# One DRAM row per token for both experts' outputs, added by the indirect stores, and the rows' steps placed anew

## The chip, the cores and the metric

The kernel runs on one core of one Trainium2 chip. The metric is device time in microseconds (us) of the whole program; the median over several executions counts. A profile is one execution taken with the hardware profiler. Its engines are PE (matrix multiply, with PEld for its weight loads), DVE (vector), ACT (scalar), POOL (GpSimd) and SP (which here only issues DMAs).

## What is computed

The input x is 16 rows of 512 tokens of 256 channels, float32. Two residual blocks follow each other; `_ln` is a layer norm without weights:

```python
x = x + _ln(attn(_ln(x)))      # an RWKV mix: three projections, a scan over the 512 tokens, a division, a projection
x = x + _ln(moe(_ln(x)))       # mixture of experts

def moe(xt):                                   # xt: 8192 tokens x 256
    scores = softmax(xt @ gate_w.T + gate_b)   # 8 experts
    top_w, top_i = top_k(scores, 2)            # two experts for each token
    y = sum over the two of top_w * expert_e(xt)           # 256 -> 256 -> 256, silu gate, biases
    z = silu(xt @ ws1.T + bs1) * (xt @ ws3.T + bs3) @ ws2.T + bs2   # the shared expert, 512 wide
    return y + z
```

## The kernel before

**Stages.** Rows b = 0 to 15 go through `front(b)` (layer norm, transposes `pt`, projections `pk`, `pv`, `pr`, the scans, the division `sb`) and `back(b)` (projection `po`, second norm, gate scores `pg`, positions `pc`). `back` ends by scattering each token's normalised row twice, once for each of its experts, into the DRAM array `xbuf`, sorted by expert: eight indirect stores from POOL at L500 per row. Each such row carries in two extra columns where its result is to go (R_TO) and its gate weight (R_GATE). `select(b)` then finds which blocks of 256 sorted rows are full; there are 71 blocks in all.

**Blocks.** A block passes a software pipeline, one stage per `push`. `block_load` reads 256 rows `xg` and the expert's weights `we` (898 KB) by SP (L589, L591). `block_turn` transposes (`px`), `block_hidden` computes `pa`, `pb`, `sil` and `he`, and `block_out` makes `pq` and `ye`. `block_store` scales `ye` by the gate on ACT (L640) and stores 2 x 128 rows by two indirect DMAs from POOL (L642) into `ybuf`, at the row that R_TO gives. `xg` has five buffers and `ye` three, so the load for a block waits until the stores of the block five ahead of it have landed. In before `ybuf` has two rows for each token, one per expert, and no store ever meets another's row; stores that belong to padding have a row number out of range and are dropped.

**The shared expert.** It runs in steps of its own (`shared`, two `hs` matrices, then `pz`). The first ten rows are done beside the row stage and go to DRAM (`zs`, written after L715 adds the bias bs2 on DVE). The last six are done in the tail.

**The tail.** After the last row come the remaining blocks, and then 32 half rows: `fetch` and `fetch_experts` read the half's `x2`, `zs` and `ybuf` rows; `gather` adds z and the two expert rows on DVE (L780, L781), takes moments, and asks POOL for the scales; `conclude` normalises on ACT and adds x2 on POOL (L792); `put` writes `out`. For the 12 halves whose z comes straight from PSUM, `add_bias` adds bs2 on POOL (L772).

**Order.** PE, DVE, ACT and SP run in an order written out by hand. Each step of a row has a place on a time axis of 10 units per row (`ROW`, with exceptions for rows 0 to 3 in `ROWS`); `BESIDE` and `PHASE` place shared steps and pushes, `Z_AFTER` and `K_LAST` place the tail's halves. All steps are sorted by place and issued so. POOL's order follows the same places through `pool` and `store`, which chain each POOL instruction behind the one ahead.

```python
at(PERIOD * b + when[n], step)          # a step of row b at its place
in_order()                              # all steps, sorted by place
```

Of the kernel before, what the change touches and what calls it, by code (L numbers as in the profile page):

```python
# [14 lines left out]
P = 128  # L15
# [14 lines left out]
PERIOD = 10.0  # L30
ROW = {'x': -8.0, 'sum': -5.0, 'sq': -2.0, 'xn': -0.5, 'pt': -0.49, 'mix': 1.0, 'r': 3.0, 'k0': 3.01, 'k1': 3.02, 'd0': 4.01, 'f0': 7.5, 'd1': 7.51, 'f1': 8.8, 'po0': 9.9, 'po1': 12.9, 'x2': 12.91, 'stc': 13.01, 'xr': 17.5, 'pu': 19.51, 'pg': 19.52, 'pc': 20.53, 'sel': 21.5}
ROWS = {1: {'x2': 13.11, 'stc': 13.21, 'xr': 17.7, 'pu': 19.71, 'pg': 19.72, 'pc': 20.73, 'sel': 21.7}, 3: {'po1': 12.4}, 0: {'k0': 2.81, 'pc': 21.53, 'sel': 21.54}, 2: {}}
CONST_AT = -4.5
# [4 lines left out]
TURN_FIRST = True  # L38
PHASE = 0.5
BESIDE = [6, 8]  # L40
EARLY = 8
LAST_BESIDE = 6
XR_COPY = 'pool'
FILL = [0.5, 0.6, 0.7, 1.5, 1.6, 2.5]
Z_AFTER = [0, 3]
K_FIRST = 1.2
K_LAST = 31.7
FINE = 1
FETCH = 4.8
FETCH_Y = 2.6  # L50
BIAS = 1.5
GATHER = -0.1
GATHER_Z = 0.1
CONCLUDE = 1.5
PUT = 2.2

# [5 lines left out]
def kernel(  # L62
# [63 lines left out]
    xbuf = dram.tile([NR, RW], F32, tag="xbuf", name="xbuf")  # L126
    ybuf = dram.tile([2 * N, C], F32, tag="ybuf", name="ybuf")


    AFTER = mybir.DependencyInfo(mybir.DependencyClass.Sync, mybir.DependencyReason.DATA)  # L130
    stored = {"x": [], "y": []}

# [64 lines left out]
    def the_constants():  # L197


        def counted(shape, pattern, name, by_partition=0):  # L200
# [12 lines left out]
        counted([P, 2], [[P, 2]], "lane", 1)  # L213
        counted([P, NT], [[2 * P, NT]], "token", 2)

        blank = const.tile([P, RW], F32, tag="blank", name="blank")
        nc.vector.memset(blank, 0.0)
        nc.vector.tensor_scalar(
            blank[:, R_TO : R_TO + 1].bitcast(U32), consts["token"][:, 0:1], float(2 * N), None, ALU.add
        )  # L220
# [162 lines left out]
    xTs = {}  # L383
    x2t = {}
    selected = {}

    def back(b):
# [32 lines left out]

        if b < B - 2:
            nc.sync.dma_start(out=x2s[b], in_=x2t.pop(b).rearrange("p t c -> p (t c)"))
        xr = []
        for k in range(2):
            r = wk.tile([P, NT, RW], F32, tag=f"xr{k}", name=f"xr{k}_{b}")
            pool(nc.gpsimd.memset(r[:, :, R_END:], 0.0))
            if k == 0:
                for t in range(NT):
                    normalise(r[:, t, 0:C], x2[:, t, :], s, t)
            pool(  # L430
                nc.gpsimd.tensor_scalar(
                    r[:, :, R_TO].bitcast(U32), consts["token"], float(2 * T * b + k), None, ALU.add
                )
            )
            xr.append(r)
# [75 lines left out]
    def select(b):  # L511
# [50 lines left out]
        if last:  # L562
# [10 lines left out]
            for e in range(E):  # L573
                for i in range(2):
                    j = nc.gpsimd.indirect_dma_start(
                        out=xbuf[:, :],
                        out_offset=bass.IndirectOffsetOnAxis(ap=padu[:, e, i : i + 1], axis=0),
                        in_=consts["blank"][:, :],
                        in_offset=None,
                    )  # L580
                    store("x", j)
        selected[b] = (atu, S, stored["x"])
        stored["x"] = []

    def block_load(atu, s, q, names):
# [50 lines left out]
    def block_store(i):  # L636

        y, xg = i["y"], i["xg"]
        for t in range(2):
            nc.scalar.mul(y[:, t, :], y[:, t, :], xg[:, t, R_GATE : R_GATE + 1])  # L640
        for t in range(2):
# [4 lines left out]
                in_offset=None,  # L646
                bounds_check=2 * N - 1,
                oob_is_err=False,
            )
            store("y", j)  # L650

# [73 lines left out]
    HOMES = (  # L725
        [("x", f"m{n}", f"{a}0") for n, a in (("r", "ek"), ("k", "ekv"), ("v", "sa"))]
        + [(f"xr{k}", n, a) for k, n, a in ((0, "d", "sb0"), (1, "xx", "ek1"))]
        + [("we", None, a) for a in ("ekv1", "sa1", "sb1")]
    )
    WAYS = len(HOMES)  # L730
    fetched = {}
    in_use = {}

    def fetch(i):
# [5 lines left out]
        cs = slice(2 * j * C, (2 * j + 2) * C)  # L740
        home, other, a = HOMES[k]
        if home == "we":
            both = wp.tile([P, WE], F32, tag="we", name=f"in{n}")
            ys, x2 = both[:, 0 : 4 * C], both[:, 4 * C : 6 * C]
        elif home == "x":
            ys = xp.tile([P, NT, C], F32, tag="x", name=f"in{n}", bufs=3).rearrange("p t c -> p (t c)")
            x2 = None
        else:
            ys = wk.tile([P, NT * RW], F32, tag=home, name=f"in{n}")[:, 0 : 4 * C]
            x2 = None  # L750
        if b in x2t:
            i["x2"] = x2t[b][:, 2 * j : 2 * j + 2, :]
        else:
            if x2 is None:
                x2 = wk.tile([P, 2 * C], F32, tag=other, name=f"inx{n}")
            nc.sync.dma_start(out=x2, in_=x2s[b][:, cs])
            i["x2"] = x2.rearrange("p (t c) -> p t c", t=2)
# [4 lines left out]
        i["ys"] = ys.rearrange("p (t k c) -> p t k c", t=2, k=2)  # L762

    def fetch_experts(i):
        b, j = i["b"], i["j"]
        mine = ybuf[2 * T * b : 2 * T * (b + 1), :].rearrange("(t p k) c -> p t k c", p=P, k=2)
        load("y", nc.sync.dma_start(out=i["ys"], in_=mine[:, 2 * j : 2 * j + 2]), stored["y"])

    def add_bias(i):
        if not i["z"]:  # L770
            y = i["ys"][:, :, 0, :]
            pool(nc.gpsimd.tensor_tensor(y, y, bs2t[:, None, :].to_broadcast([P, 2, C]), ALU.add))  # L772

    def gather(i):
# [3 lines left out]
        for p in range(parts):  # L778
            ts = slice(p * 2 // parts, (p + 1) * 2 // parts)
            nc.vector.tensor_add(acc[:, ts], i.get("pz", acc)[:, ts], ys[:, ts, 0, :])  # L780
# [4 lines left out]
            i["s"].append(scales(mv[:, :, 0], mv[:, :, 1], w, 2 // parts))  # L785

    def conclude(i):
        acc, b, j = i["acc"], i["b"], i["j"]
        if not i["fine"]:
            for t in range(2):  # L790
                normalise(acc[:, t, :], acc[:, t, :], i["s"][0], t)
            pool(nc.gpsimd.tensor_tensor(acc, acc, i["x2"], ALU.add))  # L792
            return
        for t in range(2):
            normalise(acc[:, t, :], acc[:, t, :], i["s"][t], 0)
            nc.vector.tensor_add(acc[:, t, :], acc[:, t, :], i["x2"][:, t, :])
# [239 lines left out]
```

## Time and profile before

| quantity | value |
|---|---|
| median of 6 runs | 1175.76 us (1175.6 to 1177.78) |
| the profiled execution's own time | 1171.52 us |
| its span, first to last instruction | 1169.8 us |
| mean granted PE clock | 0.957 |
| PE busy | 1073.6 us (92%) |
| DVE busy | 766.0 us (65%) |
| ACT busy | 533.7 us (46%) |
| POOL busy | 593.4 us (51%) |
| software queue (POOL's DMAs) | 37.00 MB, 8.7% of 16 engines |
| hardware queue (SP's DMAs) | 144.64 MB, 36.8% of 16 engines |

The table gives the page's first and third part. Busy shares are averages over stages that have different limits, so the text reads them stage by stage. A row of a group gives busy time and the mean of one instruction in ns; then the idle time of its engine just before, and what ended it.

### The profile page before, as it was taken

Reading aid. Unit: us, or ns where it says so; the run is one execution under the profiler, and the core shown is the slowest. Engines: PE = TensorE matmul, PEld = TensorE weight load, DVE = VectorE, ACT = ScalarE, POOL = GpSimd, SP = SyncE. Lnnn points to the kernel's source line nnn. Section 1 sums busy time; section 2 is a strip of 40 time slices with the busy share of each in tenths; the row PEclk is TensorE's granted clock in tenths of the full one; section 3 lists DMA queues with packets and bytes.
Section 4 is the critical chain, followed back from the end, with each engine's and each line's share of the span. In section 5 each row is a group of like instructions: output and inputs, shape, how many; then the busy total and the mean of one; then the engine's idle time right before and its main releaser. Section 6 shows DMA issues by size and latency. Waiting matters only on the chain.

```text
span 1169.8 us, 15070 instructions
## 1 busy us (share of the span) xinstructions
PE 1073.6 (92%) x4228; PEld 752.3 (64%) x4228; DVE 766.0 (65%) x1878; ACT 533.7 (46%) x1135; POOL 593.4 (51%) x877
## 2 busy tenths in 40 slices
PE   5678899899999999999999999999996999999993
PEld 2344565666677677767767686777665888746552
DVE  4787486877768586977769687874322222268885
ACT  3246154555637474655647464552412333333332
POOL 2235425354555546465555655554363233359897
PEclk9779899999989999999999989999987999999997
DMA  4001314334444452635445354444424666478883
GB/s 149 22 25 47 107 62 156 110 136 161 150 171 150 156 183 95 208 129 177 143 159 174 138 198 148 147 158 146 150 108 144 217 215 227 169 249 298 307 268 118
DMA packets 81124, 183.65 MB, mean 157 GB/s; under 512 B 10077, under 2 KB 44911, under 8 KB 81040
## 3 DMA queue, kind: packets, MB, share of 16 engines
q1 hardware_dynamic: 66480, 144.64, 36.8%
q0 software_dynamic: 13840, 37.00, 8.7%
q10 hardware_dynamic: 720, 1.06, 0.3%
q8 instruction: 33, 0.54, 0.2%
q14 instruction: 51, 0.42, 0.1%
HBM read 124.57 MB, written 59.92 MB: 158 GB/s over the span
## 4 chain that ended last, share of the span: by engine, by line
PE 61%; DVE 10%; POOL 9%; issue 9%; ACT 6%; DMA 2%; another core or an unknown queue 2%; SPq 0%; POOLq 0%; DVEq 0%; ACTq 0%
PE pq L629 8%; PE pa L613 8%; PE pz L703 6%; PE pb L613 6%; PE hs_pa L688 5%; PE hs_pb L688 5%; PE pr L338 5%; PE pk L338 5%; PE pv L338 4%; PE po L398 4%; PE pg L453 2%; POOL acc L792 2%; PE px L599 2%; ACT xn L270 2%
## 5 line engine op out<-in xcount | busy, mean ns | idle before, releaser
L642 POOL DMA_INDIRECT ybuf<-ye,xg x142 | 157.7, 1111 | 192.1 <-ACT ye L640 123.4
L500 POOL DMA_INDIRECT xbuf<-xr,place x128 | 128.4, 1003 | 148.0 <-DVE rest L497 101.5
L629 PE MATMUL pq<-we,he 128*128 128x256 f32 x568 | 138.6, 387 | 14.9 <-DVE he L618 14.5
L613 PE MATMUL pa<-xgT,we 128*128 128x256 f32 x568 | 134.6, 380 | 0.0
L613 PE MATMUL pb<-xgT,we 128*128 128x256 f32 x568 | 134.2, 379 | 0.0
L703 PE MATMUL pz<-ws2t,hs 128*128 128x256 f32 x512 | 125.9, 401 | 7.5 <-DVE hs L694 7.5
L618 DVE SCALAR_TENSOR_TENSOR he<-pb,we,sil 128x256 f32<-128x256 f32 x142 | 61.9, 478 | 108.0 <-PE pb L613 56.7
L616 ACT ACTIVATE sil<-pa,we 128x256 f32<-128x256 f32 x142 | 59.7, 472 | 155.2 <-PE pa L613 136.3
L629 PEld LDWEIGHTS pq<-we,he 128*128 128x128 f32 x568 | 102.4, 192 | 33.9 <-DVE he L618 20.7
L688 PE MATMUL hs_pa<-xT,ws1t 128*128 128x512 f32 x256 | 122.4, 601 | 0.3 <-ACT x L270 0.3
L703 PEld LDWEIGHTS pz<-ws2t,hs 128*128 128x128 f32 x512 | 102.2, 202 | 31.7 <-DVE hs L694 11.0
L688 PE MATMUL hs_pb<-xT,ws3t 128*128 128x512 f32 x256 | 120.4, 592 | 0.0
L613 PEld LDWEIGHTS pa<-xgT,we 128*128 128x128 f32 x568 | 108.3, 191 | 14.8
L613 PEld LDWEIGHTS pb<-xgT,we 128*128 128x128 f32 x568 | 107.9, 190 | 14.7
L371 DVE RECIPROCAL sb<-sb 128x512 f32<-128x512 f32 x32 | 107.3, 3353 | 1.1
L270 ACT ACTIVATE x<-po,nb_b,rs_b 128x256 f32<-128x256 f32 x64 | 30.9, 564 | 157.5 <-POOL nb_b L265 154.4
L688 PEld LDWEIGHTS hs_pb<-xT,ws3t 128*128 128x128 f32 x256 | 48.6, 190 | 61.5 <-issue 57.4
L245 DVE BATCH_NORM_STATS2 st_c<-x 128x6 f32<-128x256 f32 x64 | 26.3, 411 | 91.3 <-POOL x L413 90.5
L398 PE MATMUL po<-wa,g 128*128 128x256 f32 x256 | 72.9, 434 | 6.2 <-DVE g L376 6.2
L688 PEld LDWEIGHTS hs_pa<-xT,ws1t 128*128 128x128 f32 x256 | 48.7, 194 | 45.3 <-issue 42.2
L270 ACT ACTIVATE acc<-acc,nb_d,rs_d 128x256 f32<-128x256 f32 x64 | 35.1, 595 | 82.0 <-POOL nb_d L265 82.0
L633 DVE TENSOR_TENSOR ye<-pq,we 128x512 f32<-128x512 f32 x71 | 48.5, 683 | 36.7 <-PE pq L629 34.0
(179 smaller groups left out, 1928.7 us busy)
## 6 DMA issues: line engine op xcount, KB each, us to landing
we<-in_we SPq DMA_DIRECT2D x71, 898.0 KB
xg<-xbuf SPq DMA_DIRECT2D x71, 258.0 KB
in<-ybuf SPq DMA_DIRECT2D x32, 512.0 KB
x<-in_x SPq DMA_DIRECT2D x16, 512.0 KB
out<-acc SPq DMA_DIRECT2D x31, 256.0 KB
x2s<-x SPq DMA_DIRECT2D x14, 512.0 KB
zs<-z SPq DMA_DIRECT2D x10, 512.0 KB
acc<-zs SPq DMA_DIRECT2D x20, 256.0 KB
```

What stands on the lines that cost most here:

```text
L270: nc.scalar.activation(dst, src, AF.Identity, bias=nb[:, t : t + 1], scale=rs[:, t : t + 1])
L338: nc.tensor.matmul(p, w[:, c, o * P : (o + 1) * P], r, start=(c == 0), stop=(c == NC - 1))
L371: nc.vector.reciprocal(sb, sb)
L398: nc.tensor.matmul(p[:, i, :], g[:, c, t * P : (t + 1) * P], woT[:, c, :], start=(c == 0), stop=(c == NC - 1))
L500: i = nc.gpsimd.indirect_dma_start(out=xbuf[:, :], out_offset=bass.IndirectOffsetOnAxis(ap=place[:, t, k : k + 1], axis=0), in_=xr[k][:, t ...
L613: nc.tensor.matmul(p[:, f, :], w[:, k : k + P], xgT[:, c, :], start=(c == 0), stop=(c == NC - 1))
L616: nc.scalar.activation(s[:, f, :], pp[0][:, f, :], AF.Silu, bias=w[:, O_B1 + f : O_B1 + f + 1])
L618: nc.vector.scalar_tensor_tensor(h[:, f, :], pp[1][:, f, :], w[:, O_B3 + f : O_B3 + f + 1], s[:, f, :], ALU.add, ALU.mult)
L629: nc.tensor.matmul(p[:, t, :], h[:, f, t * P : (t + 1) * P], w[:, k : k + C], start=(f == 0), stop=(f == NF - 1))
L642: j = nc.gpsimd.indirect_dma_start(out=ybuf[:, :], out_offset=bass.IndirectOffsetOnAxis(ap=xg[:, t, R_TO : R_TO + 1].bitcast(U32), axis=0) ...
L688: nc.tensor.matmul(p, w[:, c, f * P : (f + 1) * P], xT[:, c, :], start=(c == 0), stop=(c == NC - 1))
L703: nc.tensor.matmul(p[:, i, :], h[f][:, t * P : (t + 1) * P], ws2t[:, f, :], start=(f == 0), stop=(f == NS - 1))
```

## The change

It gives `ybuf` one row for each token (plus 256 for padding). `clear(b)`, a new step at place 2.05 of each row, writes the bias bs2 into that row's 512 tokens by one SP DMA. The indirect stores of `block_store` no longer write but add (`compute_op=ALU.add`), and two blocks may meet in one row, so the stores of one block are ordered behind those of the block ahead, and only the two stores within a block are free of each other. The half rows then read one expert row instead of two and add it once; `add_bias` is gone, and z goes to DRAM without the bias, copied by ACT. `ROW`, `ROWS`, `BESIDE`, `PHASE`, `Z_AFTER`, `K_LAST` and `PUT` have new values. The switch `OUT_ADD` is False, so what hangs on it does not run.

```diff
-ROW = {'x': -8.0, 'sum': -5.0, 'sq': -2.0, 'xn': -0.5, 'pt': -0.49, 'mix': 1.0, 'r': 3.0, 'k0': 3.01, 'k1': 3.02, 'd0': 4.01, 'f0': 7.5, 'd1': 7.51, 'f1': 8.8, 'po0': 9.9, 'po1': 12.9, 'x2': 12.91, 'stc': 13.01, 'xr': 17.5, 'pu': 19.51, 'pg': 19.52, 'pc': 20.53, 'sel': 21.5}
-ROWS = {1: {'x2': 13.11, 'stc': 13.21, 'xr': 17.7, 'pu': 19.71, 'pg': 19.72, 'pc': 20.73, 'sel': 21.7}, 3: {'po1': 12.4}, 0: {'k0': 2.81, 'pc': 21.53, 'sel': 21.54}, 2: {}}
+ROW = {'x': -7.5, 'sum': -4.5, 'sq': -2.0, 'xn': -0.5, 'pt': -0.49, 'mix': 1.0, 'r': 3.5, 'k0': 3.01, 'k1': 3.02, 'd0': 4.01, 'f0': 7.5, 'd1': 7.51, 'f1': 8.8, 'po0': 11.9, 'po1': 12.9, 'x2': 12.91, 'stc': 12.92, 'xr': 17.5, 'pu': 19.51, 'pg': 19.72, 'pc': 20.73, 'sel': 21.7}
+ROWS = {1: {'x': -8.3, 'sum': -5.5, 'sq': -2.5, 'xn': -1.0, 'pt': -0.99, 'r': 5.5, 'd0': 5.51, 'x2': 13.11, 'stc': 13.21, 'xr': 17.7, 'pu': 19.71}, 3: {'po1': 12.4, 'x2': 12.41}, 0: {'xn': 0.0, 'pt': 0.01, 'k0': 2.81, 'pc': 21.53, 'sel': 21.54}, 2: {}}
...
-PHASE = 0.5
-BESIDE = [6, 8]
+PHASE = 0.2
+BESIDE = [5, 9, 3]
...
-Z_AFTER = [0, 3]
+Z_AFTER = [2, 3]
...
-K_LAST = 31.7
+K_LAST = 32.2
...
-BIAS = 1.5
+OUT_ADD = False
+CLEAR_AT = 2.05
...
-PUT = 2.2
+PUT = 2.0
...
-    ybuf = dram.tile([2 * N, C], F32, tag="ybuf", name="ybuf")
+    ybuf = dram.tile([N + BS, C], F32, tag="ybuf", name="ybuf")
...
+    def clear(b):
+
+        todo = [ybuf[T * b : T * (b + 1), :]] + ([ybuf[N:, :]] if b == 0 else [])
+        for a in todo:
+            n = a.shape[0] // P
+            i = nc.sync.dma_start(out=rows(a), in_=bs2t[:, None, :].to_broadcast([P, n, C]))
+            for g in adds:
+                tc.declare_no_dep(i.ins, group=g, reason="rows of no earlier block")
...
     def block_store(i):
 
         y, xg = i["y"], i["xg"]
+
+        adds.append(f"y_adds{i['q']}")
...
-                bounds_check=2 * N - 1,
-                oob_is_err=False,
+                compute_op=ALU.add,
             )
-            store("y", j)
+            store(None, j)
+            tc.declare_no_dep(j.ins, group=adds[-1], reason="tokens of their own")
+            tc.add_to_no_dep_group(adds[-1], j.ins)
...
-            nc.vector.tensor_tensor(
-                z[b][:, 2 * j : 2 * j + 2, :], p, bs2t[:, None, :].to_broadcast([P, 2, C]), ALU.add
-            )
+            nc.scalar.copy(z[b][:, 2 * j : 2 * j + 2, :], p)
...
-        mine = ybuf[2 * T * b : 2 * T * (b + 1), :].rearrange("(t p k) c -> p t k c", p=P, k=2)
-        load("y", nc.sync.dma_start(out=i["ys"], in_=mine[:, 2 * j : 2 * j + 2]), stored["y"])
-
-    def add_bias(i):
-        if not i["z"]:
-            y = i["ys"][:, :, 0, :]
-            pool(nc.gpsimd.tensor_tensor(y, y, bs2t[:, None, :].to_broadcast([P, 2, C]), ALU.add))
+        mine = rows(ybuf[T * b : T * (b + 1), :])
+        nc.sync.dma_start(out=i["ys"], in_=mine[:, 2 * j : 2 * j + 2])
...
-            nc.vector.tensor_add(acc[:, ts], i.get("pz", acc)[:, ts], ys[:, ts, 0, :])
-            nc.vector.tensor_add(acc[:, ts], acc[:, ts], ys[:, ts, 1, :])
+            nc.vector.tensor_add(acc[:, ts], i.get("pz", acc)[:, ts], ys[:, ts])
...
+        at(PERIOD * b + CLEAR_AT, lambda b=b: clear(b))
```

More of the change, by code (lines that the diff above doesn't have):

```diff
@@ L38 @@
 TURN_FIRST = True
-PHASE = 0.5
-BESIDE = [6, 8]
+PHASE = 0.2
+BESIDE = [5, 9, 3]
 EARLY = 8
 LAST_BESIDE = 6
-XR_COPY = 'pool'
+XR_COPY = "pool"
 FILL = [0.5, 0.6, 0.7, 1.5, 1.6, 2.5]
-Z_AFTER = [0, 3]
+Z_AFTER = [2, 3]
 K_FIRST = 1.2
-K_LAST = 31.7
+K_LAST = 32.2
 FINE = 1
@@ L126 @@
     xbuf = dram.tile([NR, RW], F32, tag="xbuf", name="xbuf")
-    ybuf = dram.tile([2 * N, C], F32, tag="ybuf", name="ybuf")
+    ybuf = dram.tile([N + BS, C], F32, tag="ybuf", name="ybuf")
     AFTER = mybir.DependencyInfo(mybir.DependencyClass.Sync, mybir.DependencyReason.DATA)
-    stored = {"x": [], "y": []}
+    stored = {"x": []}
+    adds = []
     BEHIND = mybir.DependencyInfo(mybir.DependencyClass.NoSync, mybir.DependencyReason.DATA)
@@ L147, in store @@
             tail["stores"].append(ins.ins.name)
+        if what is None:
+            return
         tc.declare_no_dep(ins.ins, group=f"{what}_stores", reason="rows of their own")
@@ L213, in the_constants @@
         counted([P, 2], [[P, 2]], "lane", 1)
-        counted([P, NT], [[2 * P, NT]], "token", 2)
-        blank = const.tile([P, RW], F32, tag="blank", name="blank")
+        counted([P, NT], [[P, NT]], "token", 1)
+        blank = const.tile([P, BS // P, RW], F32, tag="blank", name="blank")
         nc.vector.memset(blank, 0.0)
         nc.vector.tensor_scalar(
-            blank[:, R_TO : R_TO + 1].bitcast(U32), consts["token"][:, 0:1], float(2 * N), None, ALU.add
+            blank[:, :, R_TO].bitcast(U32), consts["token"][:, 0 : BS // P], float(N), None, ALU.add
         )
@@ L384 @@
     x2t = {}
+    kept = {}
     selected = {}
@@ L419, in back @@
         yield
-        if b < B - 2:
+        if OUT_ADD:
+            kept[b] = nc.sync.dma_start(out=rows(out[b]), in_=x2t.pop(b)).ins.name
+        elif b < B - 2:
             nc.sync.dma_start(out=x2s[b], in_=x2t.pop(b).rearrange("p t c -> p (t c)"))
@@ L431, in back @@
                 nc.gpsimd.tensor_scalar(
-                    r[:, :, R_TO].bitcast(U32), consts["token"], float(2 * T * b + k), None, ALU.add
+                    r[:, :, R_TO].bitcast(U32), consts["token"], float(T * b), None, ALU.add
                 )
@@ L577, in select @@
                         out_offset=bass.IndirectOffsetOnAxis(ap=padu[:, e, i : i + 1], axis=0),
-                        in_=consts["blank"][:, :],
+                        in_=consts["blank"][:, i, :],
                         in_offset=None,
@@ L725 @@
     HOMES = (
-        [("x", f"m{n}", f"{a}0") for n, a in (("r", "ek"), ("k", "ekv"), ("v", "sa"))]
-        + [(f"xr{k}", n, a) for k, n, a in ((0, "d", "sb0"), (1, "xx", "ek1"))]
-        + [("we", None, a) for a in ("ekv1", "sa1", "sb1")]
+        [("x", f"{a}0") for a in ("ek", "ekv", "sa")]
+        + [("xr0", "sb0"), ("xr1", "ek1")]
+        + [("we", a) for a in ("ekv1", "sa1", "sb1")]
     )
     WAYS = len(HOMES)
-    fetched = {}
     in_use = {}
@@ L740, in fetch @@
         cs = slice(2 * j * C, (2 * j + 2) * C)
-        home, other, a = HOMES[k]
+        home, a = HOMES[k]
         if home == "we":
             both = wp.tile([P, WE], F32, tag="we", name=f"in{n}")
-            ys, x2 = both[:, 0 : 4 * C], both[:, 4 * C : 6 * C]
         elif home == "x":
-            ys = xp.tile([P, NT, C], F32, tag="x", name=f"in{n}", bufs=3).rearrange("p t c -> p (t c)")
-            x2 = None
-        else:
-            ys = wk.tile([P, NT * RW], F32, tag=home, name=f"in{n}")[:, 0 : 4 * C]
-            x2 = None
+            both = xp.tile([P, NT, C], F32, tag="x", name=f"in{n}", bufs=3).rearrange("p t c -> p (t c)")
+        else:
+            both = wk.tile([P, NT * RW], F32, tag=home, name=f"in{n}")
+        two = both[:, 0 : 4 * C].rearrange("p (n t c) -> p n t c", n=2, t=2)
+        i["ys"] = two[:, 0]
         if b in x2t:
             i["x2"] = x2t[b][:, 2 * j : 2 * j + 2, :]
[L753 to L757, printed above, removed]
+        elif not OUT_ADD:
+            i["x2"] = two[:, 1]
+            nc.sync.dma_start(out=both[:, 2 * C : 4 * C], in_=x2s[b][:, cs])
         acc = wk.tile([P, 2 * C], F32, tag=a, name=f"acc{n}")
@@ L761, in fetch @@
         i["acc"] = acc.rearrange("p (t c) -> p t c", t=2)
-        i["ys"] = ys.rearrange("p (t k c) -> p t k c", t=2, k=2)
     def fetch_experts(i):
         b, j = i["b"], i["j"]
-        mine = ybuf[2 * T * b : 2 * T * (b + 1), :].rearrange("(t p k) c -> p t k c", p=P, k=2)
-        load("y", nc.sync.dma_start(out=i["ys"], in_=mine[:, 2 * j : 2 * j + 2]), stored["y"])
-    def add_bias(i):
-        if not i["z"]:
-            y = i["ys"][:, :, 0, :]
-            pool(nc.gpsimd.tensor_tensor(y, y, bs2t[:, None, :].to_broadcast([P, 2, C]), ALU.add))
+        mine = rows(ybuf[T * b : T * (b + 1), :])
+        nc.sync.dma_start(out=i["ys"], in_=mine[:, 2 * j : 2 * j + 2])
     def gather(i):
@@ L785, in gather, with onto @@
             i["s"].append(scales(mv[:, :, 0], mv[:, :, 1], w, 2 // parts))
+    def onto(i, t):
+        b, j = i["b"], i["j"]
+        ts = slice(2 * j + t.start, 2 * j + t.stop)
+        d = nc.gpsimd.dma_start(out=rows(out[b])[:, ts], in_=i["acc"][:, t], accum_op=ALU.add)
+        tc.add_manual_dep(d.ins, kept[b], AFTER, reason="what it adds to")
+        pool(d)
     def conclude(i):
@@ L791, in conclude @@
                 normalise(acc[:, t, :], acc[:, t, :], i["s"][0], t)
-            pool(nc.gpsimd.tensor_tensor(acc, acc, i["x2"], ALU.add))
+            if not OUT_ADD:
+                pool(nc.gpsimd.tensor_tensor(acc, acc, i["x2"], ALU.add))
             return
@@ L795, in conclude @@
             normalise(acc[:, t, :], acc[:, t, :], i["s"][t], 0)
-            nc.vector.tensor_add(acc[:, t, :], acc[:, t, :], i["x2"][:, t, :])
-            nc.sync.dma_start(out=rows(out[b])[:, 2 * j + t], in_=acc[:, t, :])
+            if OUT_ADD:
+                onto(i, slice(t, t + 1))
+            else:
+                nc.vector.tensor_add(acc[:, t, :], acc[:, t, :], i["x2"][:, t, :])
+                nc.sync.dma_start(out=rows(out[b])[:, 2 * j + t], in_=acc[:, t, :])
     def put(i):
@@ L801, in put @@
         if not i["fine"]:
-            nc.sync.dma_start(out=rows(out[b])[:, 2 * j : 2 * j + 2], in_=i["acc"])
+            if OUT_ADD:
+                onto(i, slice(0, 2))
+            else:
+                nc.sync.dma_start(out=rows(out[b])[:, 2 * j : 2 * j + 2], in_=i["acc"])
         del in_use[i["k"] % WAYS]
@@ L888, in blank_block @@
             out=rows(xbuf[E * STRETCH :, :]),
-            in_=consts["blank"][:, None, :].to_broadcast([P, BS // P, RW]),
+            in_=consts["blank"],
         )
@@ L945 @@
             halves.append((n, dict(b=rows_done + r, j=f - NS, z=False)))
-    kept = [(b, j) for b in range(rows_done) for j in range(NT // 2)]
-    for i, (b, j) in enumerate(kept):
-        halves.append((K_FIRST + (K_LAST - K_FIRST) * i / (len(kept) - 1), dict(b=b, j=j, z=True)))
+    spilt = [(b, j) for b in range(rows_done) for j in range(NT // 2)]
+    for i, (b, j) in enumerate(spilt):
+        halves.append((K_FIRST + (K_LAST - K_FIRST) * i / (len(spilt) - 1), dict(b=b, j=j, z=True)))
     halves.sort(key=lambda h: h[0])
@@ L958 @@
         at(max(n - FETCH_Y, free, 0.001) + 0.001, lambda i=i: fetch_experts(i))
-        at(max(n - BIAS, free, 0.001) + 0.002, lambda i=i: add_bias(i))
         at(n + (GATHER_Z if not i["z"] else GATHER), lambda i=i: gather(i))
```

## The prediction

> **What bounds the kernel now.** I read the page first, then the busy times cut by stage, because the shares of the whole span mix stages with different limits. Columns: stretch, its length, busy time (instructions) of PE, PEld, DVE, ACT, POOL; granted PE clock; DMA share; GB/s.
>
> ```profile
> 0.00:60.00 60.00, 34.64 (x80) 16.93 (x80) 35.79 (x72) 20.66 (x52) 15.30 (x46) 0.89 0.28 90
> ...
> 60.00:115.00 55.00, 46.04 (x138) 26.50 (x139) 45.69 (x84) 28.97 (x66) 24.89 (x44) 0.83 0.08 31
> ...
> 537.00:590.00 53.00, 51.90 (x237) 39.58 (x235) 39.54 (x100) 29.72 (x66) 28.10 (x41) 1.00 0.47 160
> ...
> 890.00:995.00 105.00, 102.46 (x477) 85.29 (x476) 27.44 (x51) 36.08 (x82) 31.21 (x32) 0.99 0.62 213
> ...
> 1140.00:1170.00 30.00, 10.58 (x39) 8.00 (x37) 15.85 (x34) 7.82 (x14) 21.00 (x36) 0.75 0.38 122
> ```
>
> PE is the limit in a middle row (51.9 of 53) and in the block stretch of the tail (102.5 of 105). It isn't at the start (34.6 of 60) and at the end (10.6 of 30, where POOL has 21). So time can be won by removing PE's waits in the rows, by a shorter start, and by a shorter end. It can be lost where stores pace the blocks. PE's waits in the full rows (220 to 870 us) are almost all at one place:
>
> ```profile
> PE pc L481 <- DVE sc L476: 9.1, 9, 1.2
> PE pc L481 <- DVE mine L475: 2.7, 1, 2.7
> ```
>
> For SP, the list of waits in the block stretch (915 to 1025) names the stores:
>
> ```profile
> SPq L589 <- DMA ybuf<-ye,xg: 49.9, 13, 5.5
> ```
>
> Then the timeline of that stretch, which is where the change adds its wait:
>
> ```profile
> 941.09 0.97 POOL L642 DMA_INDIRECT ybuf<-ye,xg  x1 [3.83 <-ACT ye L640]
> ...
> 942.37 0.97 POOL L642 DMA_INDIRECT ybuf<-ye,xg  x1 [0.30 <-issue]
> ...
> 946.30 0.38 SPq L589 DMA_DIRECT2D xg<-xbuf  x1
> ...
> 947.17 0.97 POOL L642 DMA_INDIRECT ybuf<-ye,xg  x1 [3.83 <-ACT ye L640]
> ...
> 948.45 0.98 POOL L642 DMA_INDIRECT ybuf<-ye,xg  x1 [0.31 <-issue]
> ...
> 953.09 0.38 SPq L589 DMA_DIRECT2D xg<-xbuf  x1
> ```
>
> POOL issues a block's two stores in 2.25 us (941.09 to 943.34), then idles 3.83 us: blocks come every 6.08 us. SP's next `xg` load goes out when those stores have landed, so its issue dates the landing: 2.96 us after the stores' issue ended, then 3.66. The eleven such distances from 939.66 to 1003.42 run from 2.4 to 6.6 and average 4.1.
>
> Last the timeline of the end:
>
> ```profile
> 1143.35 0.70 PE L703 MATMUL pz<-ws2t,hs 128*128 128x256 f32 x2 [1.04 <-DVE hs L694]
> ...
> 1147.70 7.57 PE L703 MATMUL pz<-ws2t,hs 128*128 128x256 f32 x26 [3.64 <-DVE hs L694]
> ...
> 1154.43 1.26 POOL L772 TENSOR_TENSOR in<-in,bs2t 128x512 f32<-128x512 f32 x1
> ...
> 1155.72 0.42 DVE L780 TENSOR_TENSOR acc<-pz,in 128x256 f32<-128x256 f32 x1 [1.18 <-POOL in L772]
> ...
> 1162.04 0.83 DVE L796 TENSOR_TENSOR acc<-acc,x 128x256 f32<-128x256 f32 x1 [1.02 <-ACT acc L270]
> ```
>
> PE waits for a DVE that is behind, and the last half then waits for POOL's bias add. PE ends at 1155.27, the last add at 1162.87.
>
> **The rows: pc (gain).** In the order before, only the eight `po` matmuls of step po0 (1.97 us) stand between `pg` and `pc`, and `pc` waits about 1 us for DVE's chain in nine rows. With po0 moved from 9.9 to 11.9, a shared step stands there in every later row: four `hs_pa` and four `hs_pb` (1.72 + 1.72 us) or 16 `pz` (3.45 us), so 1.5 us more cover than po0 gave, against waits of up to 1.2. The last row's 2.7 us wait, which has nothing between, gets 16 `pz` too. Both rows together bound the gain at 11.8 us. Next late is DVE (39.5 of 53 busy in such a row). PE's other data waits in 220 to 870 sum to only 2.6 us, so there is little to inherit, but moved steps can create new ones. I take 7 of 11.8; bounds 0 and 11.8.
>
> **The ramp: r behind k0, k1 (gain).** Step r is eight matmuls (3.43 us, the row "pr L338 x8" of the chain) and two Exp on ACT (598 ns each). At the start the chain of waits runs PE `pr`, PE `pk`, then DVE `ekv`, two scans, two divisions, PE `po`. With r behind k1, `ekv` of the second half comes 3.43 us sooner in row 0 and again in row 1. `er` is wanted only by the second instruction of the division, which follows two scans (1.2 us each), so r's 3.43 us lie beside them only in part. I take 3.4 in all; bounds 6.9 gained and 3.4 lost, should `er` become the late one.
>
> **Moved steps that I cost at nothing.** x (one 512 KB load on SP) and sum (eight ACT instructions and one POOL mean) go half a unit later, earlier in row 1. Cover is ACT's idle half (29.7 of 53); if gone, sum costs ACT 2.4 us (412 ns x 4 and 197 ns x 4). stc only passes nothing of weight. pg and sel move 0.2 units: 8 to 25 small DVE instructions of 0.2 us, and with sel the pushes, hence SP's loads, POOL's stores. BESIDE and PHASE shift shared steps (1.72 + 1.72 us of PE) between rows without changing their number. `clear`: 17 DMAs from SP, nearest row the 512 KB zs writes, 0.33 to 0.45 us to issue, into DMA engines that are 0.47 busy; without that cover 512 KB at the 394 GB/s peak seen in the tail is 1.3 us each. The z copy takes 20 DVE instructions of 671 ns away (13.4 us) and gives ACT 20 of about 587 ns (the `xgT` copy's row, same shape). ACT now waits for `pz` where DVE did, with `xn` and `hs_s` queued behind it; cover is again ACT's idle half, 0.6 us each if gone. In the rows, two blocks' stores follow each other within 0.6 to 1.2 us of POOL time once a row; there the new wait holds POOL for about 1 us, and behind it stand `xr` and `rs_a`, where POOL waits 86.6 us in 15 times for ACT `xn` anyway.
>
> **The tail's blocks: the wait for the adds (loss).** Behind a waiting store POOL has only later stores; who waits for it is SP, for the `xg` buffer, and so PE's `px`. Wait alone: 2.25 us to issue plus about 4.0 to land (4.1 less SP's register work) is 6.25. SP's loads already go at (1003.42 - 920.90) / 13 = 6.35 us, since stores land behind the weight loads that they themselves released. So the wait alone adds nothing to that loop. The add must also read its destination. The page's software queue took 8.7% of 1169.8 us for 286 stores, 0.36 us each; doubling that adds 0.36 for the second store, the first one's lying under the second's issue. No row shows an adding DMA. Lower bound 0; upper bound a second full landing, 4 us. I take 0.36, nearest to the queue's own row. Loads then fall behind PE by 6.35 + 0.36 - 6.08 = 0.63 us a block, 8.2 us in 13 blocks. The cover: the load issued at 920.90 is used by `px` at 928.95 (8.05 us), one issued at 974.21 is used at 977.58 without a stall (3.37 us), so 4.7 us are to spare. Cost 8.2 - 4.7 = 3.5.
>
> The Trainium skill ("DMA: Bandwidth & Descriptors", Anatomy of one DMA) gives the software path a fixed cost of about 2.0 us, most of it the write receipt. By it, stores would be through in some 4.6 us of 6.08, and the term would be 0; the 2.4 to 6.6 us of the rows, under load, disagree, and I go by the rows. Against the change speaks "Collectives: The Full Stack" (the bandwidth ceiling): an adding DMA is slower for its second read, by about half the rate; no run here shows it yet.
>
> **The end (gain).** Of the 33 `acc` adds at L781 (33.6 us of DVE after 1022) and the 12 bias adds at L772 (16.6 us of POOL) nothing is left, and 32 reads shrink from 512 to 256 KB, 8.4 MB. From 1100 to 1147.7 PE idles 6.0 us (4.31 in 1100 to 1146, 1.7 after) because DVE is 39.5 of 46 busy there; with 33 us less in the tail I take 5.0 of it. PE's end to the last add is 7.6 us; without L781 (0.42 + 1.12) and without waiting for L772 (0.45), less what Z_AFTER and K_LAST push later, I take 1.7 off. Sum 6.7; bounds 1.7 and 8.5.
>
> **Sum.** 7 + 3.4 + 6.7 - 3.5 = 13.6 off the profiled 1171.5: 1157.9. The median of the runs stands 4.2 above the profiled execution, so 1162.
>
> **Rivals.**
> - The adds pace the tail (slower). Place: the 13 loads between 920 and 1003. If an add lands e us later than a plain store, the cost is 13 x (0.27 + e) - 4.7; it eats the gains of 17.1 from e = 1.4. At e = 2.5 it is 31.3, so 14 us slower: 1190. For it: stores already land up to 6.6 us late, and nothing shows an add. Against: the queue is 8.7% busy.
> - The end stays: the last halves hang on DMA or SP, not on DVE and POOL. Without the 6.7: 1168.6. For it: DMA share 0.82 to 0.86 in 1060 to 1146. Against: the rows above name DVE and POOL.
> - Moved steps make new waits of 1 us in 13 rows where I have gains (no 7, no 3.4, 13 lost instead): 1185.5; at half of those 13, 1179. For it: rows are 97% full. Against: the PE waits that they remove are seen.
> - That stores aren't really ordered can't be: in the build each block's first store names the software queue's counter of the block ahead.
>
> **Chances.** Forecast 0.55 (1152 to 1168); end stays 0.13; adds pace 0.20; new waits 0.12. About 0.2% (2.4 us) is what a measurement here can tell from no change. Faster 0.55 + 0.13 + 0.02 = 0.70; same 0.05; slower 0.19 + 0.06 = 0.25. The range goes from 1152 (pc and end at their bounds) to 1184 (e up to about 2).
>
> **What would show it.** Right: PE's wait for `pc` gone from the list; `ekv` before `pr` in row 0; in the block stretch POOL's idle before a store ended by the stores' own DMA, yet `px` still every 6.1 us; POOL without L772 and PE's end about 5 us nearer to the span's. Wrong: `px` at 7 us or more per block, PE waiting for `xg` there; or new PE waits in the rows above 10 us.

## The result, and the profile after

The changed kernel takes 1183.37 us (median of 20 runs, 1180.16 to 1192.43) against 1175.7 us for the kernel before (44 runs): ratio 1.0073, 95% interval 1.0061 to 1.0086. It is 0.7% slower; 1162 was forecast. The profiled execution took 1193.01 us (span 1190.6), just above the slowest of these runs. In later comparisons the changed kernel came out at 1179.93 and 1180.69, while the kernel before took 1174.89 in one and 1157.55 to 1158.66 in three others (the record has a chip of its own for each of the four). So the ratio depends on what the kernel before does there (1.004 [1.0023, 1.0057] and 1.0197 [1.0169, 1.0224]), but the sign never does.

Busy times by stage, with the stretches of before moved to the same work (columns as before):

```profile
0.00:60.00 60.00, 36.23 (x88) 18.11 (x88) 40.61 (x77) 24.16 (x62) 17.80 (x51) 0.91 0.37 121
...
535.00:586.00 51.00, 50.94 (x230) 39.03 (x229) 38.45 (x101) 32.42 (x68) 30.32 (x40) 1.00 0.60 162
900.00:1005.00 105.00, 82.09 (x379) 69.09 (x378) 19.50 (x37) 29.76 (x68) 38.20 (x25) 0.95 0.65 174
...
1160.00:1191.00 31.00, 18.57 (x76) 13.93 (x74) 14.76 (x36) 8.93 (x17) 18.79 (x39) 0.87 0.33 110
```

The middle row is denser (50.94 of 51), and the end has PE work in it (18.57 of 31, before 10.58 of 30). The block stretch has gone the other way: PE works 82 of 105 us, before 102.5. PE's waits name the cause, first in the full rows (217 to 870), then in the block stretch (900 to 1039); the columns are us in total, times, longest:

```profile
PE px L617 <- DMA xg<-xbuf: 4.8, 3, 2.2
PE pa L631 <- ACT x L276: 4.8, 3, 2.6
PE px L617 <- ACT x L276: 3.6, 2, 2.5
...
PE px L617 <- DMA xg<-xbuf: 30.1, 15, 4.6
```

`pc` has left the list of the rows, but waits for ACT's normalise and for `xg` have come in. In the block stretch PE waits 30 us for gathered rows, and SP's list says what holds their loads (915 to 1025):

```profile
SPq L607 <- DMA ybuf<-ye,xg: 74.3, 16, 7.6
```

The timeline of POOL, ACT, SP and PE over one block of that stretch:

```profile
939.95 1.54 POOL L662 DMA_INDIRECT ybuf<-ye,xg  x1 [3.78 <-ACT sil L634]
941.80 1.54 POOL L662 DMA_INDIRECT ybuf<-ye,xg  x1 [0.30 <-issue]
947.13 1.54 POOL L662 DMA_INDIRECT ybuf<-ye,xg  x1 [3.79 <-ACT sil L634]
...
940.07 0.90 ACT L660 ACTIVATE ye<-ye,xg 128x256 f32<-128x256 f32 x2
...
946.53 0.38 SPq L607 DMA_DIRECT2D xg<-xbuf  x1
...
942.29 0.63 PE L617 MATMUL px<-ident,xg 128*128 128x128 f32 x4 [1.26 <-DMA xg<-xbuf]
949.44 0.63 PE L617 MATMUL px<-ident,xg 128*128 128x128 f32 x4 [1.34 <-DMA xg<-xbuf]
```

An adding store keeps POOL busy for 1.54 us, where a plain one took 0.97. A pair so takes 3.39 us (939.95 to 943.34), not 2.25. POOL then idles 3.79 us. `sil`, printed there as releaser, is not what the next pair waits for: its rows were scaled on ACT by 940.97, 6.2 us before it goes out at 947.13. The landing of the pair ahead is dated by SP's load at 946.53, 0.6 us before. (With the new places and without the wait, e4 below, a pair goes out 0.33 us after its first half's rows are scaled.) Issue and landing so stand in a ring: 7.2 us here, while PE needs 6.08 per block. Two lines of the page show the price of the adds, the software queue and the group of the stores:

```profile
q0 software_dynamic: 27472, 38.83, 16.0%
...
L662 POOL DMA_INDIRECT ybuf<-ye,xg x142 | 231.7, 1631 | 280.5 <-issue 69.1
```

Before, they were 13840 packets and 8.7%, and 157.7 us at 1111 ns. The 13632 packets more are 96 for each of the 142 stores. The queue's share nearly doubles at almost the same bytes.

Stages of the profiles; "row 15" is the start of `pg` of the last row, "tail" the time from the first to the last of the tail's 18 `px`, "block" the mean of its last 13 intervals, "end" the time from the last `px` to the span's end (all us). The ratio is to the kernel before in the same comparison; e1 to e4 ran in one, e5 and e8 to e10 in a second, e6 and e11 to e13 in a third, f1 to f4 in a fourth. e2 and e8 also clear both rows of each token, 1024 KB per row of the batch (not 2 MB, as the expectation of e2 has it); e1, e5 and the changed kernel clear 512 KB.

| kernel | row 15 | tail | block | end | ratio |
|---|---|---|---|---|---|
| before | 844.2 | 105.9 | 6.08 | 161.8 | 1 |
| e4 new places alone | 818.6 | 107.8 | 6.08 | 163.7 | 0.9831 |
| e3 old places, wait | 844.1 | 119.3 | 7.11 | 161.4 | 1.0080 |
| e2 old places, add and clears | 852.3 | 107.8 | 6.21 | 160.1 | 1.0062 |
| e5 old places, the rest of the change | 858.8 | 131.3 | 7.95 | 160.9 | 1.0308 |
| e1 new places, one row, wait | 826.6 | 121.2 | 6.77 | 150.9 | 0.9876 |
| e8 new places, add and clears | 844.3 | 107.0 | 6.17 | 163.5 | 0.9956 |
| e12 new places, POOL delayed | 835.7 | 107.5 | 6.08 | 163.9 | 1.0003 |
| changed kernel | 846.4 | 138.1 | 7.92 | 152.4 | 1.0073 |
| e10 changed kernel again | 838.7 | 137.3 | 8.08 | 152.3 | 1.0040 |
| f1 changed kernel again | 843.9 | 135.2 | 7.53 | 152.7 | 1.0197 |
| f2 = e4 beside f1 | 820.1 | 107.8 | 6.08 | 163.7 | 0.9843 |

### The profile page after: what moved, and what is told of

Read it like the earlier page. It is cut to its first block, busy times and chain, and to the rows that moved or that the text cites. A ratio compares the mean times of both kernels' runs of the same rounds, so it can differ in the third digit from the quotient of the medians.

```text
span 1190.6 us, 14978 instructions
## 1 busy us (share of the span) xinstructions
PE 1073.7 (90%) x4228; PEld 754.2 (63%) x4228; DVE 722.2 (61%) x1825; ACT 562.1 (47%) x1169; POOL 643.4 (54%) x865
## 5 line engine op out<-in xcount | busy, mean ns | idle before, releaser
L662 POOL DMA_INDIRECT ybuf<-ye,xg x142 | 231.7, 1631 | 280.5 <-issue 69.1
L647 PE MATMUL pq<-we,he 128*128 128x256 f32 x568 | 142.9, 397 | 4.0 <-DVE he L636 3.5
L631 PE MATMUL pa<-xgT,we 128*128 128x256 f32 x568 | 137.1, 385 | 4.8 <-ACT x L276 4.8
L724 PE MATMUL pz<-ws2t,hs 128*128 128x256 f32 x512 | 123.3, 397 | 12.9 <-DVE hs L715 12.2
L709 PE MATMUL hs_pa<-xT,ws1t 128*128 128x512 f32 x256 | 125.6, 614 | 0.0
L724 PEld LDWEIGHTS pz<-ws2t,hs 128*128 128x128 f32 x512 | 101.6, 200 | 35.2 <-DVE hs L715 12.9
L647 PEld LDWEIGHTS pq<-we,he 128*128 128x128 f32 x568 | 106.6, 198 | 19.8 <-DVE he L636 5.5
L715 DVE SCALAR_TENSOR_TENSOR hs<-hs_pb,colt,hs_s 128x512 f32<-128x512 f32 x64 | 45.8, 720 | 65.9 <-PE hs_pb L709 30.5
L617 PE MATMUL px<-ident,xg 128*128 128x128 f32 x284 | 44.0, 278 | 39.3 <-DMA xg<-xbuf 34.9
```

What stands on the lines that cost most here:

```text
L617: nc.tensor.transpose(p[:, c, t * P : (t + 1) * P], xg[:, t, c * P : (c + 1) * P], ident)
L631: nc.tensor.matmul(p[:, f, :], w[:, k : k + P], xgT[:, c, :], start=(c == 0), stop=(c == NC - 1))
L647: nc.tensor.matmul(p[:, t, :], h[:, f, t * P : (t + 1) * P], w[:, k : k + C], start=(f == 0), stop=(f == NF - 1))
L662: j = nc.gpsimd.indirect_dma_start(out=ybuf[:, :], out_offset=bass.IndirectOffsetOnAxis(ap=xg[:, t, R_TO : R_TO + 1].bitcast(U32), axis=0) ...
L709: nc.tensor.matmul(p, w[:, c, f * P : (f + 1) * P], xT[:, c, :], start=(c == 0), stop=(c == NC - 1))
L715: nc.vector.scalar_tensor_tensor(h[f], pp[1], colt[:, C_S3 + f : C_S3 + f + 1], s, ALU.add, ALU.mult)
```

## The experiments

The theory after the result: the adds are dear on POOL (1.54 us of issue) and, ordered block behind block, pace the tail. Rivals: the wait alone does it, whatever is stored; or the new places cost the time.

**e1: plain stores in the changed kernel.**

```diff
                 in_offset=None,
-                compute_op=ALU.add,
             )
```

> The changed kernel with plain stores in place of the adding ones: the later expert's row overwrites the earlier one's, so the sum is left out; the wait of each block's stores for those of the block ahead stays, and so do the single row per token and the new places. Theory A (the wait is late because an add is dearer than a plain store: 1.54 us of POOL's issue against 0.97, 1 KB packets, later landing; wait and add only hurt together): the tail's 18 px go back from 138 us to 106-112, the total falls to about 1152-1164. Theory B (the wait on the block ahead is what costs, whatever is stored): the tail stays at 130-138 us and the total at 1178-1188. Theory C (the new places of the rows' steps cost it): also 1178-1188.

Measured: 1143.57 us, ratio 0.9876 [0.9862, 0.9890]. The new places are not what costs. The tail is 121.2 us, between the two theories: without adds 17 us of the 32 are gone, but 15 stay. Its timeline shows the ring with plain stores:

```profile
939.43 0.96 POOL L662 DMA_INDIRECT ybuf<-ye,xg  x1 [4.32 <-issue]
940.69 0.96 POOL L662 DMA_INDIRECT ybuf<-ye,xg  x1 [0.30 <-ACT ye L660]
946.12 0.96 POOL L662 DMA_INDIRECT ybuf<-ye,xg  x1 [4.48 <-issue]
```

2.22 us of issue and 4.5 of idling make 6.7, already over 6.08.

**e2: adds without the wait, in the kernel before** (each onto its own cleared row).

```diff
+                compute_op=ALU.add,
             )
             store("y", j)
...
+        at(PERIOD * b + 2.05, lambda b=b: clear(b))
```

> The kernel before with adding stores, each expert's output onto a row of its own that was cleared to the bias (so the bias is in the output once too often), one clear of 2 MB per row of the batch, and no wait between blocks. Theory A (add and wait only together): POOL issues a pair in 3.4 us of a period of 6.1, the tail lengthens by 0-6 us, total 1175-1184. Theory A2 (the add alone paces the tail, through the later release of the gathered rows): tail 125-138 us, total 1195-1210. Theory B (wait alone): tail 106 us, total 1174-1179.

Measured: 1166.27 us, ratio 1.0062 [1.0040, 1.0083]. The tail stays at 107.8 us. The 8 us are lost in the rows, which no theory had priced; whether to the adds or to the 16 MB of clears that this run also has, it does not tell.

**e3: the wait without adds, in the kernel before.** The two stores of a block get a group of their own, so they are ordered behind the block ahead.

```diff
-        tc.declare_no_dep(ins.ins, group=f"{what}_stores", reason="rows of their own")
+        group = group or f"{what}_stores"
+        tc.declare_no_dep(ins.ins, group=group, reason="rows of their own")
...
-            store("y", j)
+            store("y", j, group=f"y_stores{i['q']}")
```

> The kernel before, plain stores into two rows per token, each block's stores made to wait for those of the block ahead. Theory A or A2: the pair's 2.25 us and some 2.5 us of landing fit into the period of 6.1 us, tail 106-109 us, total 1174-1180. Theory B (the wait by itself): tail 125-138 us, total 1195-1210.

Measured: 1167.35 us, ratio 1.0080 [1.0066, 1.0095]. The tail is 119.3 us, the rows are unchanged to 0.1 us. So theory A, that plain stores with the wait would fit into 6.08 us, falls: the wait alone costs 13 us of tail, and the add adds to it.

**e4: the new places alone.** The kernel before with the changed kernel's `ROW`, `ROWS`, `PHASE`, `BESIDE`, `Z_AFTER`, `K_LAST` and `PUT`.

> The kernel before with the changed kernel's places of the rows' steps and of the end alone; stores, bias adds and fetches as before. If the 2 us that the rows gained come from the places: 1171-1175, with the end of before (some 162 us behind the last px). If the end's gain of 9 us came from the places (K_LAST, PUT, BESIDE) and not from the removed fetches and bias adds: 1162-1168. If the places cost time that the lighter end hides: 1178-1185.

Measured: 1136.86 us, ratio 0.9831 [0.9818, 0.9845], a gain none of the three guesses had. Row 15 comes 25.6 us sooner, the end is no shorter. Run twice more (e13: 1140.57, 0.9848 [0.9825, 0.9871]; f2: 1139.27, 0.9843 [0.9820, 0.9867]) it holds. PE's waits in its rows (210 to 818) are nearly none:

```profile
PE pg L453 <- ACT xT L438: 1.3, 2, 1.0
PE pq L629 <- DVE he L618: 1.0, 4, 0.4
PE pt L276 <- ACT xn L270: 0.3, 2, 0.2
```

**e5: the changed kernel with the old places**; e10: the changed kernel again beside it.

> The changed kernel with the places of the kernel before. Theory A (the places are worth 1.7% and adds with their waits cost some 2.4%, each by itself): ratio to before 1.020-1.028 less the end's gain already in it, so near 1.024, pg of row 15 at 860-875 us. Theory B (with the adds the places are worth nothing): ratio 1.005-1.010.

Measured: 1210.6 us, ratio 1.0308 [1.0274, 1.0342], above both guesses, and e10 1.004. The places are worth some 2.6% with the adds as well. Row 15 comes at 858.8 us. The end is 160.9 us here: the lighter end gains 1 us at the old places, the new places alone lose 2 (e4), and both together gain 9.

**e8: adds without the wait, at the new places.**

> The kernel with the new places alone, and in it adding stores onto rows of their own, cleared to the bias, with no wait between blocks (the bias is in the output once too often). If the add costs what it did at the old places (8 us, nearly all in the rows): ratio to before 0.988-0.992, tail 106-110 us. If the new places leave POOL less room for 1.54 us instead of 0.97 per store: 1.000 or more, pg of row 15 at 838-846 us.

Measured: 1169.5 us, ratio 0.9956 [0.9941, 0.9972], between the two; row 15 comes at 844.3 us, as in the second. In the rows the adds and their clears together take back the whole 25.6 us that the places gave (e4 stood in another comparison), while the tail keeps 6.17 us per block. PE's longest wait in its rows is for gathered rows:

```profile
PE px L605 <- DMA xg<-xbuf: 15.1, 6, 5.1
```

**e12: only POOL's time.** e4, with plain stores and no wait; behind each store POOL copies a scratch tile.

```diff
             store("y", j)
+            pool(nc.gpsimd.tensor_copy(consts["dummy"], consts["dummy"]))
```

> The kernel with the new places alone, plain stores, no wait; behind each store POOL copies a scratch tile of 128x512 onto itself, some 0.55 us by its 128x1024 copy of 1.05 us, about what an add's issue takes more than a plain store's (1.54 against 0.97 us). If POOL's time is what an add costs in the rows: ratio to before 0.993-0.998 as with the adding stores without a wait (0.9956), PE's waits for xg in the rows near 15 us. If the transfer itself (1 KB packets, later landing) is what costs: 0.983-0.986.

Measured: 1159.32 us, ratio 1.0003 [0.9987, 1.0019], above both guesses and 0.0155 above e13 beside it. Time on POOL alone, with no DMA more, costs the rows 17 us (818.7 to 835.7). Its waits go another way than e8's, though: not `xg` but ACT's normalise, which waits for POOL's `nb_b`. The lines are the copy's group (208 to 836), then PE's and ACT's waits there:

```profile
L653 POOL COPY dummy<-dummy 128x512 f32<-128x512 f32 x96 | 61.3, 639 | 0.8
...
PE pa L615 <- ACT x L272: 5.0, 7, 1.8
...
ACT x L272 <- POOL nb_b L267: 139.5, 12, 12.9
```

In f2 that last wait is 110.8 us, in f1 129.4. The copy takes 0.64 us, the add 0.57 more than a plain store, so this dose is a little larger than the add's.

**e9: a try to get the end's gain with plain stores.** At the new places, bs2 is added to each expert's own bias and the bias adds at the end go. The expectation was wrong on the sum: a token's two gates come from a softmax over all eight experts and do not sum to one, so the output holds bs2 scaled by their sum, and the kernel serves for its time only.

```diff
+        nc.vector.tensor_add(w[:, O_B2 : O_B2 + C], w[:, O_B2 : O_B2 + C], bs2t)
...
-        at(max(n - BIAS, free, 0.001) + 0.002, lambda i=i: add_bias(i))
```

> A version meant to beat both: the new places and plain stores into two rows per token, with the shared bias added to each expert's own bias (the two gates of a token sum to one), so that POOL's bias adds at the end go and z is copied by ACT. If the end's gain of 9-12 us came from POOL's bias adds: ratio 0.970-0.976. If it came from the halved fetches of one row per token: 0.983 as the new places alone.

Measured: 1153.45 us, ratio 0.9839 [0.9814, 0.9865]. The end falls from 163.7 to 156.4 us, so POOL's bias adds are the larger part of what a lighter end gives. But row 15 comes at 830.8, 12 us behind e4's, and nothing is won over e4; whether that is the one more DVE add per block or the z copy that went from DVE to ACT was not separated.

**Four kernels beside each other (f1 to f4).** Because the kernel before differs by 1.5% between comparisons, the changed kernel, the places alone, and two variants of the changed kernel ran together. The variants had run before as e11 (1171.69 us, ratio 1.0113) and e6 (1203.53, 1.0394).

> The changed kernel, beside the next three. If adds and waits cost what the stages of the two profiles say (rows 20-28 us, tail 30 us, less 11 us at the end): some 3-4% above the places alone.

Measured: 1180.69 us against 1139.27 for f2: 41.4 us, 3.6%. By stage 23.8 us in the rows, 3.2 up to the first tail `px`, 27.4 in the tail, 11.0 won at the end: 43.4 of the spans' 43.5.

f3, the clears ahead of all adds:

```diff
-        at(PERIOD * b + CLEAR_AT, lambda b=b: clear(b))
+        at(PERIOD * (1 + b // 8) + CLEAR_AT + 0.9 * (b % 8), lambda b=b: clear(b))
```

> The changed kernel with the clears ahead of all adds. If the adds' 6-10 us of waits for a clear are on the path: 5-10 us below the changed kernel on this chip, gained in the rows. If they fall into slack: within 2 us of it.

Measured: 1175.92 us, 4.8 below f1, just short of the first guess. Row 15 comes at 830.8 us, 13.1 sooner, of which the tail (138.4) gives 3 back in this profile. So the clears' place is part of the rows' loss. It is not by the adds' waits for a clear: these are 10.3 us in 4 times in the first profile, but 1.5 us in one in f1. By what else, no run shows.

f4, six buffers for gathered rows:

```diff
-        xg = wp.tile([P, 2, R_END], F32, tag="xg", name=f"xg{q}", bufs=4 + LEAD)
+        xg = wp.tile([P, 2, R_END], F32, tag="xg", name=f"xg{q}", bufs=5 + LEAD)
```

> The changed kernel with six buffers for gathered rows in place of five. If the tail is paced by the chain of add, landing, next add (a rate, some 7.5 us per block): the tail stays at 130-138 us and the ratio at 1.000-1.006. If it is paced by the load that waits for a buffer (a latency): the tail falls to 106-120 us and the ratio to 0.985-0.992.

> The changed kernel with six buffers of gathered rows. If the first run's loss is the kernel's own: 20-30 us above the changed kernel on this chip, lost in the rows (pg of row 15 near 865 us), the tail at 130 us again. If it was the chip's: within 5 us of it.

Measured: 1210.34 us, ratio 1.043 [1.0384, 1.0475], 28 to 30 us above f1 (e6: 1203.53). The tail keeps its rate, 7.64 us per block in e6 and 8.20 in f4: what paces it is the ring of adds, not the load's latency. Row 15 at 861.2 us repeats e6's 864.7. From row 3 to row 15 PE idles no longer than in f1 (16.4 against 16.7 us); its waits only move, to `pt` behind ACT's `xn`. The 20 us more are the same 2600 matmuls, busy for 630.3 us at a granted clock of 0.96, where f1 has 610.1 at 0.99. The end is 8 us longer too (160.5). Why earlier loads should bring that is not settled; the order of instructions on every engine is the same in both.

## Why the prediction was wrong

**The tail's blocks are the step that failed; the first rival named the right place.** The term was +3.5 us; the profiles show +32.2 (105.9 to 138.1). It was priced as a ring of 2.25 us issue, 4.0 landing and 0.36 for the second read. Three things are wrong in it. That the stated range, up to 1184, holds the result is the rival's part in it; the forecast was a gain.

- The issue. An add was taken to cost POOL what a plain store costs. It costs 1.54 against 0.97 us, and both of a pair stand in the ring: 1.14 us per block, the largest omission, and nothing in the trace of before showed it. It belonged in the range from the start: "no row shows an adding DMA" was applied to the landing only.
- The wait by itself. It was set at 6.25 us, inside the load's loop of 6.35 ("So the wait alone adds nothing to that loop"). e3 measures 7.11 us per block and e1 6.77, with idle times of 3.5 to 7.2 us between the pairs of their tails. A store also lands later once ordered: median 5.8 us from issue in e3's tail against 3.9 in e4's (4.4 in f2).
- The sum. In the changed kernel 3.39 us of issue and 4.1 to 4.7 of idling behind it make the 7.5 to 8.1 us of the profiles (7.92, 8.08, 7.53), where 6.71 was forecast. The idling is no longer than with plain ordered stores (4.55 in e1, 4.86 in e3), so in the ring the add costs its issue, and the 0.36 for a second read does not show there. Of the 28.7 us missed, 15.7 are 13 blocks at 7.92 instead of 6.71, 8.2 are the first four intervals (35 us against 27) and 4.7 the cover, which was not there.

The rival's formula, 13 x (0.27 + e) - 4.7, gives these 32 us at e = 2.5, the very case it priced ("At e = 2.5 it is 31.3, so 14 us slower: 1190"). That is in part luck: e was to be a later landing, while the block's excess over 6.35 us is only 1.2 to 1.7, mostly issue, and the first four intervals fill the gap. Why they are slow is not shown.

So neither add nor wait explains it alone: the adds alone leave the tail at 107 us (e8), the wait alone brings 119 to 121 (e1, e3), both 131 (e5, old places) to 138.

**The rows: a gain too small and a loss left out.** Places: pc -7 (bound 11.8) and ramp -3.4 (bound 6.9) were forecast, 10.4 together; e4 shows 25.6, of which 10.7 come by row 3. The same matmuls lie up to row 3's `pg` in before, e4 and e1 (columns as in the busy times above):

```profile
0.00:219.60 219.60, 175.29 (x537) 101.39 (x537) 155.17 (x342) 95.55 (x216) 79.59 (x156) 0.89 0.23 80
...
0.00:208.90 208.90, 166.75 (x536) 98.16 (x536) 155.32 (x342) 95.39 (x216) 81.78 (x156) 0.92 0.25 84
...
0.00:216.90 216.90, 174.48 (x536) 103.50 (x536) 154.99 (x340) 98.00 (x220) 80.84 (x156) 0.88 0.28 95
```

From there to row 15's `pg` in before, e4, e1, the changed kernel and f3:

```profile
219.60:844.10 624.50, 611.61 (x2600) 448.22 (x2600) 455.05 (x1195) 335.37 (x717) 332.89 (x476) 0.99 0.46 156
...
208.90:818.60 609.70, 605.69 (x2601) 445.83 (x2601) 453.91 (x1195) 353.86 (x731) 328.84 (x476) 0.99 0.48 161
...
216.90:826.60 609.70, 605.69 (x2601) 445.81 (x2601) 445.99 (x1180) 360.19 (x743) 322.32 (x476) 0.99 0.52 169
...
216.90:846.40 629.50, 612.15 (x2601) 447.26 (x2601) 447.06 (x1180) 359.21 (x743) 380.86 (x476) 0.99 0.60 163
...
214.50:830.80 616.30, 607.44 (x2600) 442.81 (x2600) 448.96 (x1180) 358.70 (x743) 383.20 (x476) 1.00 0.57 157
```

The waits were priced about right. From row 3 on PE's idle time falls by 8.9 us (12.9 to 4.0), and the wait for `pc` was 9.1 of it. In the ramp it falls by only 2.1 us (44.3 to 42.2; by 4.8 in f2): the waits for `po` (6.2 us) and for `pr` behind `mr` (5.9) shrink to 0.3 and none, but longer or new ones for `xn`, `xr` and `pc` take most of that back. The rest, 8.5 us in the ramp (2.8 in f2) and 5.9 after it, is less PE time for the same matmuls, in the ramp of e4 at a granted clock of 0.92 instead of 0.89. The prediction had no term for that, and no run shows what sets it.

Loss: the rows' wait was put at 1 us on POOL with nothing on PE, the clears were covered by idle DMA engines, and the add's longer issue did not occur. e1 has the wait, the clears and the z copy, and from row 3 on PE's time in it is e4's to 0.1 us: with plain stores, these three cost nothing there, as forecast. (Row 15 comes 8 us later than in e4 because of the ramp, 216.9 against 208.9 us, where PE idles alike and is busy longer at a granted clock of 0.88.) The changed kernel differs from e1 by the adds alone and takes 629.5 us there (623.0 in e10, 626.8 in f1), so the adds cost the rows 13 to 20 us (f1 against f2 beside it: 18.7). With the clears ahead it takes 616.3 us (f3, and the same in e11), so all but 7 or 8 us of this needs the clears in their place as well. In e8, with clears twice as large, adds and clears take 25.7 us in all; POOL's time without any transfer takes 17 (e12). The changed kernel's row 15 lands at 838.7 to 846.4 us, about where it was before. The sum of gain and loss in the first profile, -2.0 up to the first tail `px`, looks like a small miss and is two large ones.

**The end: the right way, beyond its bound.** -6.7 was forecast with bounds to -8.5; -9.4 is measured. But e5 (-0.9) and e4 (+1.9) show that it takes the lighter end and the new `Z_AFTER`, `K_LAST` and `PUT` together; the prediction credited the removed instructions alone and counted the new places against them.

**Sum by the steps:** -2.0 (rows and last stretch), +32.2, -9.4 give +20.8, the distance of the two profiled spans (1169.8 to 1190.6). The medians differ by 7.7, as the changed kernel's profiled run is 9.6 above its median and before's 4.2 below.

**The other rivals.** "New waits" named the right place, the full rows, but blamed the moved steps; it was the stores. "The end stays" is out (its time is 1168.8 by the prediction's own terms, not 1168.6). What the text gave as a sign of being wrong, `px` at 7 us or more and PE waiting for `xg`, is what came.

The Trainium skill's passage that spoke against the change ("Collectives: The Full Stack", the bandwidth ceiling) says of a ReduceScatter that it is slower because its add needs two source reads. The runs agree as to direction (queue share 8.7 to 16.0%), though here the packets also get smaller, and the larger costs were POOL's issue and the ring. The fixed cost of about 2.0 us for the software path ("DMA: Bandwidth & Descriptors", Anatomy of one DMA) would have made the tail's term 0; idle times of 3.4 to 7.7 us between ordered pairs disagree with it here.

**What stays open.** How the adds reach PE in the rows is argued, not shown: PE waits for gathered rows in e8, for ACT behind POOL in e12, for both in the changed kernel, and why the clears' place matters so much is open. Nor is it known why the kernel before takes 1158 us in some comparisons and 1175 in others. The difference lies in one stretch: e3, run beside a 1158, reaches row 15 at the same time, but the first tail `px` 45.3 us later where before's profile has 57.9. The next `he` of DVE there, in before's profile and in e3:

```profile
886.86 0.88 DVE L618 SCALAR_TENSOR_TENSOR he<-pb,we,sil 128x256 f32<-128x256 f32 x2 [21.90 <-remote]
...
865.07 0.88 DVE L619 SCALAR_TENSOR_TENSOR he<-pb,we,sil 128x256 f32<-128x256 f32 x2 [0.30 <-ACT sil L617]
```

DVE stands still for 21.9 us, ACT twice for over 12, and the profile names no instruction that ended DVE's wait; the order of instructions on every engine is the same in both. The four profiles beside the 1174.89 (e5, e8, e9, e10) have 52.9 to 56.7 us in this stretch, the twelve beside the three others 44.9 to 51.1, so it goes with the comparison, not with the change.

**The version that beats both** is the new places alone with two rows per token: 0.983 to 0.985 of the kernel before where that takes 1158 us (it was not run beside a 1175), and 3.5% below the changed kernel beside it (1139.27 / 1180.69).

## What to carry to other kernels

When stores become ordered, write down the ring (issue of all of a block's stores, plus their landing under load) and compare it with the consumer's period; here rings of 6.8 to 8.1 us paced a loop of 6.08 while the queue was 9 to 16% busy. Price a new kind of DMA on the engine that issues it too: POOL's chain of instructions was half idle here, and 0.64 us per store still reached the limiting engine through the small steps queued behind (e12). When a change bundles new places with new traffic, run the places alone first; here they held a gain that the rest consumed. And when a stage's time moves, split it into the engine's idle and busy time first; here 14 of 25.6 us were busy time of the same matmuls.

## What the hardware showed that was not expected

- An indirect store that adds occupies POOL for 1.54 us per 128 rows of 1 KB, a plain one for 0.97 (medians of the tail, 1543 and 972 ns), although both move the same 128 KB.
- Its data go out in four times as many packets, 128 of 1 KB for 32 of 4 KB in the traces: 96 more per store (13632 over 142). The queue's share of the DMA engines rises from 8.9 to 16.3% between e4 and e8, at 37.0 MB in both.
- Plain stores land 1.1 to 1.9 us later, counted from their issue, when each pair waits for the pair ahead (median over the tail 5.5 in e1 and 5.8 in e3 against 3.9 in e4 and 4.4 in f2).
- The same 2600 matmuls between rows 3 and 15 kept PE busy for 603.9 us (f2) to 630.3 us (f4), at granted clocks of 0.99 and 0.96.
